# Value products of an attention kernel in 64-row tiles, put between the score products

## The chip, the cores and the metric

The kernel runs on one core of a Trainium2 chip. The metric is the device time of one execution in microseconds (us), the median of three runs. Profiled numbers come from one further execution, recorded by the hardware profiler.

## The reference, cut to what matters

One pre-norm transformer block on x of shape (8, 1024, 512), all float32: a differential attention and then a feed-forward part, each added to its input.

```python
# attention: b = 8, s = 1024, H = 16 heads, HD = 32
qkv = layernorm(x) @ w_qkv                       # (b, s, 1536)
q1, q2 = halves of q over d; k1, k2 likewise     # 16 numbers each
a1 = softmax(q1 @ k1.T * scale);  a2 = softmax(q2 @ k2.T * scale)
out = (a1 - lam * a2) @ v                        # per head, lam one number
out = out / rms(out) * norm_w * (1 - 0.8)
x = x + out.reshape(...) @ wo
# feed-forward, 512 -> 2048 -> 512; bitlinear: weights -1, 0, 1 with a scale for each row
y = layernorm(x)
h = bitlinear(y, w_fc) + gate * (y @ v.T @ fast_b.T @ u.T)
x = x + bitlinear(relu(h) ** 2, w_proj)
```

## The kernel before, in words

**Units and steps.** The attention is cut into 256 units: a batch entry, a head, and one half of the 1024 queries. A unit has 8 chunks `kc` of 128 keys, and the main loop (line 594) takes two chunks in a step, so a unit has four steps, with `kc` 0, 2, 4 and 6. The loop runs in an order written out by hand: `tc.manual_schedule` keeps each engine's instructions in the order in which the code gives them.

**What a step computes.** Both softmaxes of the differential attention are kept side by side: map 0 in rows 0 to 63 of the tiles of keys and queries, map 1 in rows 64 to 127. (The 16 numbers of a half head are split into high and low parts, which is how 64 rows come about.)

- `max_scores` (line 197) multiplies scores of a unit 16 chunks ahead, two products of 64 rows by 128 columns, into two of the three banks of `ps_mx`; VectorE reduces each bank to its row maximum (line 218, tile `nm`). A step has two such calls, so four products and four reductions.
- `exp_scores` (line 253) computes the scores of the present unit, transposed, keys by queries. For each map it takes two products into one bank: the negative maxima, spread by `one2` (tiles `nms`), and then keys by queries (`tk`, `tq`). ScalarE takes the exponential into `e` (line 273). A step has two such calls. The banks come from `ps_1` (tag `one`), which has four.
- `values` (line 296) multiplies the exponentials of the step before with the values `v`: four products side by side for each chunk, each 128 rows (keys) by 32 columns (the head's 32 numbers), for two maps and two quarters of queries, all in the one bank `acc`, which accumulates over the 8 chunks. `quarters` (line 287) issues them. The operands are plain float32, and each such product stands in the trace as two weight loads and two matmuls, so that the two calls of a step give 16 matmuls of `acc`.
- `evict` (line 305) brings a finished `acc` to `avs` with one ScalarE instruction, which also multiplies the rows of map 1 with minus lambda.

GpSimd adds the exponentials up (`add_up`, lines 283 and 285) for the softmax denominators.

**Work of 128 rows.** In the step with `kc` 0 there is more: `max_turn` (one transpose of the maxima, line 232, then two VectorE copies and DMAs to `nms`), `heads_out` (four transposes of `avs` of an earlier unit, line 324, then five VectorE instructions, lines 334 to 347), `sums` (the denominators, 16 matmuls of 128 rows by 32 columns through `quarters`, tile `one` from `es`), and mostly one piece of preparation for the next batch entry: `project` (8 matmuls of 128x128 by 512, line 157, then ScalarE line 164, VectorE line 165 and a store), `value_tile` (8 such matmuls, line 145, then ScalarE) or `turn_tile` (4 transposes). One step with `kc` 4 in four units has `output_rows` (line 383). All of these take a bank of `ps_1`.

**Order in a step, before.** TensorE does all score products, then the work of 128 rows, then the two `values` calls; what the other engines do with the results of the 128-row work (the `posts`) comes last, and `evict` comes at the start of the step after.

**Feed-forward.** After the units, four output banks `y` from `ps_1` and a work bank from `ps_acc` serve the feed-forward part.

Of the kernel before, what the change touches and what calls it, by code (L numbers as in the profile page):

```python
# [8 lines left out]
F32 = mybir.dt.float32  # L9
F32R = mybir.dt.float32r  # L10
AF = mybir.ActivationFunctionType
ALU = mybir.AluOpType
# [5 lines left out]
P = 128  # L18
# [6 lines left out]
def block_phases(  # L25
# [14 lines left out]
    nc = tc.nc  # L40
# [16 lines left out]
    p_tq = ctx.enter_context(tc.tile_pool(name="a_tq", bufs=5))  # L57
    wpool = ctx.enter_context(tc.tile_pool(name="a_w", bufs=1))
    ps_mx = ctx.enter_context(tc.tile_pool(name="a_ps_mx", bufs=3, space=PSUM))
    ps_1 = ctx.enter_context(tc.tile_pool(name="a_ps_1", bufs=4, space=PSUM))  # L60
    ps_acc = ctx.enter_context(tc.tile_pool(name="a_ps_acc", bufs=1, space=PSUM))

    wqk = big.tile([P, KC, 2 * E], F32, tag="wqk", name="wqk")
# [166 lines left out]
    def max_turn(u):  # L230
        tr = one_bank()
        nc.tensor.transpose(tr[0:8, 0:P], nm2_of.pop(u), ident)

        def post():
            mt = p_s.tile([8, 2, P], F32R, tag="mt", name="mt", bufs=2)
            nc.vector.tensor_copy(mt[:, 0, :], tr[0:8, 0:P])
            nc.vector.tensor_sub(mt[:, 1, :], tr[0:8, 0:P], mt[:, 0, :].bitcast(F32))
            md = dpool.tile([2, 4, 2, P], F32, tag="md", name="md", bufs=4)
            nc.sync.dma_start(md.rearrange("s c a t -> (s c) a t"), mt.bitcast(F32))
            for sm in range(2):  # L240
                nc.sync.dma_start(
                    nms[u % 3][64 * sm : 64 * sm + 2].bitcast(F32)
                    .rearrange("a (c t) -> a c t", c=4),
                    md[sm].rearrange("c a t -> a c t"),
                )

        return post
# [5 lines left out]
    def exp_scores(u, kc, between=None):  # L253


        if kc % 2 == 0:
            e_of[u, kc // 2] = p_e.tile([P, 2, 2, HS], F32, tag="e", name="e")
        e = e_of[u, kc // 2]
        halves = (1, 0) if between else (0, 1)
        st = {sm: one_bank() for sm in halves}  # L260
        for w, m, cols in (
            (one2, nms[u % 3], slice(0, P)),
            (tk_of[u // 2], tq_of[u], slice(kc * P, (kc + 1) * P)),
        ):
            for sm in halves:
                rows = slice(64 * sm, 64 * sm + 64)
                nc.tensor.matmul(  # L267
                    st[sm], w[rows, cols], m[rows, :], start=(w is one2), stop=(w is not one2)
                )
        if between:  # L270
            between()
        for sm in halves:
            nc.scalar.activation(e[:, kc % 2, sm, :], st[sm], AF.Exp)  # L273
# [13 lines left out]
    def quarters(out, w, e, start, stop):  # L287

        for g in range(4):
            nc.tensor.matmul(  # L290
                out[32 * g : 32 * g + 32, :], w,
                e[:, g // 2, (g % 2) * (HS // 2) : (g % 2 + 1) * (HS // 2)],
                start=start, stop=stop,
            )

    def values(u, kc):
        b, h = divmod(u // 2, H)
        if kc == 0:
            acc_of[u] = ps_acc.tile([P, 512], F32, tag="acc", name="acc")[:, 0 : HS // 2]
        quarters(  # L300
            acc_of[u], v_of[b][:, kc, h * HD : (h + 1) * HD], e_of[u, kc // 2][:, kc % 2],
            kc == 0, kc == NS - 1,
        )

    def evict(u):
        avs_of[u] = p_s.tile([P, 2, HS // 2], F32, tag="avs", name="avs", bufs=4)

        nc.scalar.activation(avs_of[u][:, 0, :], acc_of.pop(u), AF.Copy, scale=one_nlam)

    def sums(u):  # L310
        ps = one_bank()
# [121 lines left out]
    def whole(step):  # L433
        post = step()
        if post:
            post()
# [151 lines left out]
    for v in range(NU):  # L588
        adds.setdefault((v + 1, 2) if light(v) else (v + 2, 0), []).append(v)
        outs.setdefault((v + 2, 0) if light(v) else (v + 3, 0), []).append(v)  # L590
    done = None
    ctx.enter_context(tc.manual_schedule(engines=engines))
    with tc.tile_pool(name="a_e", bufs=5) as p_e, tc.tile_pool(name="a_es", bufs=2) as p_es:
        for s in range(0, NS * NU + 2, 2):
            u, kc = divmod(s, NS)
            um, im = divmod(s + AHEAD, NS)
            if done is not None:
                evict(done)
                done = None
            if u > NU - 2 * H and kc == 0:  # L600
                prep.fetch()
            if u == NU - 1 and kc == 0:

                m1 = nms[(NU - 3) % 3].rearrange("p (k r) -> p k r", k=KC)
                nc.sync.dma_start(
                    m1.bitcast(F32), prep.m1_d.rearrange("p k i r -> p k (i r)")
                )
            if um < NU:
                if im == 0 and um + 1 < NU:
                    if um % 2 == 1:  # L610
                        load_keys(um // 2 + 1)
                    load_queries(um + 1)
                between, first = max_scores(um, im, apart=True)
            else:
                between = first = None
            if u < NU:
                if u % (2 * H) == 0 and kc == 0:
                    assert not fill
                    fill = prepare(u // (2 * H) + 1) if u + 2 * H < NU else prepare_tokens()
                exp_scores(u, kc, between=between)  # L620
                if first:
                    first()
                exp_scores(u, kc + 1)
                add_up(u, kc)
            reduce = max_scores(um, im + 1) if um < NU else None
            posts = []

            if fill and (kc == 0 or kc == 4 and u % (2 * H) >= H and u % 4 == 0):
                prepare_step, long = fill.pop(0)
            else:  # L630
                prepare_step = None
            if prepare_step and long:
                posts.append(prepare_step())
            if kc == 0 and um <= NU:
                posts.append(max_turn(um - 1))
            for v in outs.pop((u, kc), []):
                posts.append(heads_out(v))
                if v % 4 == 3:
                    n = v // 4
                    later[u, 6] = lambda n=n: rms_squares(n)  # L640
                    later[u + 1, 0] = lambda n=n: rms_sums(n)
                    later[u + 1, 2] = lambda n=n: rms_apply(n)
                    later[u + 2, 4] = lambda n=n: output_rows(n)
            if (u, kc) in later:
                posts.append(later.pop((u, kc))())
            for v in adds.pop((u, kc), []):
                posts.append(sums(v))
            if prepare_step and not long:
                posts.append(prepare_step())
            if reduce:  # L650
                reduce()
            if 2 <= s < NS * NU + 2:
                uv, kv = divmod(s - 2, NS)
                values(uv, kv)
                values(uv, kv + 1)
                if kv == NS - 2:
                    done = uv
            for post in posts:
                if post:
                    post()  # L660
        evict(done)
        whole(lambda: sums(NU - 1))
    assert not later and list(adds.values()) == list(outs.values()) == [[NU - 1]]

# [45 lines left out]
        )  # L710

    def work_bank():
        return ps_acc.tile([P, 512], F32, tag="acc", name="wb")

    def turn(g, i):
        tr = work_bank().rearrange("p (k t) -> p k t", k=KC)
# [80 lines left out]
    for k in range(NG * NJ + LAG):  # L797
        g, j = divmod(k, NJ)
        if g < NG:
            if g + 1 < NG and j == 6:  # L800
                load(g + 1)
            if g + 1 < NG and 7 <= j < 9:
                stats(g + 1, 2 * j - 14)
                stats(g + 1, 2 * j - 13)
            if g + 1 < NG and 10 <= j < 14:
                center(g + 1, j - 10)
            post = hidden(g, j)
            if k == 0:
                first = post
            else:  # L810
                if k == 1:

                    r2_of[0] = first()
                r2_of[k] = post()
            if ends:
                ends.pop(0)()
            if k in rest:
                whole(rest.pop(k))
            if g + 1 < NG and 11 <= j < 15:
                turn(g + 1, j - 11)  # L820
            if g + 1 < NG and j == 15:
                low_rank(g + 1)
        if k >= LAG:
            gc, jc = divmod(k - LAG, NJ)
            if jc == 0:
                y_of[gc] = [ps_1.tile([P, E], F32, tag="one", name="y") for _ in range(4)]
            if k < NG * NJ:
                contract(y_of[gc], jc, r2_of.pop(k - LAG))
                if jc == NJ - 1:
                    output(gc, y_of.pop(gc))  # L830
# [283 lines left out]
```

## Time and profile before

| | |
|---|---|
| median of three runs | 5339.66 us (5339.15 to 5343.71) |
| span of the profiled execution | 5338.5 us |
| granted TensorE clock | 0.999 |
| TensorE matmul busy | 5280.1 us, 99% of the span |
| VectorE, ScalarE, GpSimd busy | 3787.7, 2832.5, 4121.0 us |
| matmuls of `acc` (line 290) | 16384, 1092.7 us busy |
| maxima (line 218), VectorE | 4096 of 683 ns |
| first and last score product of `max_scores` | 56.2 and 4226.5 us |

The profile lists busy time by engine, the chain of work that ended last, groups of instructions by source line, and a timeline. In the groups, "64*128 64x512" means a weight tile of 64 rows by 128 columns, through which 512 columns are streamed. PE is TensorE's matmuls, PEld its weight loads, DVE VectorE, ACT ScalarE, POOL GpSimd. A matmul's recorded duration includes its way through the array, so matmuls overlap in the record, and the distances between their starts say more than their durations.

### The profile page before, as it was taken

How to read it: one execution, taken by the hardware profiler on the slowest of the kernel's cores; microseconds unless marked ns; L12 is line 12 of the kernel's file. 1: busy time of each engine (PE TensorE's matmuls, PEld its weight loads, DVE VectorE, ACT ScalarE, POOL GpSimd, SP SyncE). 2: the span in 40 equal slices, each digit the busy share in tenths (PEclk: the TensorE clock that was granted, in tenths of full speed). 3: DMA queues.
4: the chain of work that ended last, by engine and by line, in shares of the span. 5: the costliest groups of instructions: out<-in, count | busy, mean ns of one | idle time of the engine just before them, and what ended most of it. 6: DMA issues, size and time to landing. Idle time of an engine off the chain costs nothing.

```text
span 5338.5 us, 105587 instructions
## 1 busy us (share of the span) xinstructions
PE 5280.1 (99%) x41522; PEld 3243.9 (61%) x41522; DVE 3787.7 (71%) x7599; ACT 2832.5 (53%) x5502; POOL 4121.0 (77%) x1495
## 2 busy tenths in 40 slices
PE   8999999999999999999999999999999999999999
PEld 4555555555555555555555555555555578888887
DVE  6877787777778777877777777777888645555554
ACT  4665566566656665666566656655666522222221
POOL 0898899889988998899899989998888733333333
PEclk9999999999999999999999999999999999999999
DMA  8112211211121112111211121112211101111111
GB/s 275 47 55 74 71 50 55 75 66 55 54 77 65 52 57 77 64 55 56 75 65 50 60 81 57 56 61 78 100 48 44 50 31 32 32 32 32 32 32 32
DMA packets 185246, 328.48 MB, mean 62 GB/s; under 512 B 33312, under 2 KB 55840, under 8 KB 184112
## 3 DMA queue, kind: packets, MB, share of 16 engines
q1 hardware_dynamic: 183824, 319.12, 18.3%
q8 instruction: 329, 5.39, 0.4%
q0 software_dynamic: 544, 2.10, 0.1%
q14 instruction: 165, 1.35, 0.1%
q10 hardware_dynamic: 384, 0.52, 0.0%
HBM read 209.16 MB, written 112.46 MB: 60 GB/s over the span
## 4 chain that ended last, share of the span: by engine, by line
PE 84%; POOL 11%; DVE 3%; issue 1%; ACT 1%; DMA 0%; SPq 0%; POOLq 0%; DVEq 0%; ACTq 0%
PE acc L290 15%; PE one L267 14%; PE mx L207 13%; PE y L763 9%; PE pf L744 8%; PE one L157 8%; POOL es L285 6%; PE one L290 4%; PE one L145 4%; PE one L383 3%; POOL es L283 3%; PE one L324 2%; DVE nm L218 1%; PE pf L748 1%; POOL ss L369 1%
## 5 line engine op out<-in xcount | busy, mean ns | idle before, releaser
L218 DVE TENSOR_REDUCE nm<-mx 128x1 f32<-128x512 f32 x4096 | 2550.3, 683 | 256.6 <-PE mx L207 251.5
L273 ACT ACTIVATE e<-one 128x512 f32<-128x512 f32 x4096 | 2116.5, 603 | 803.2 <-PE one L267 751.1
L285 POOL TENSOR_TENSOR es<-es,e 128x2048 f32<-128x2048 f32 x495 | 2261.3, 4568 | 63.2 <-ACT e L273 31.1
L207 PE MATMUL mx<-tk,tq 64*128 64x512 f32 x4096 | 1453.1, 444 | 6.2 <-DVE nm L218 5.6
L283 POOL TENSOR_TENSOR es<-e 128x2048 f32<-128x2048 f32 x256 | 1169.6, 4569 | 278.3 <-ACT e L273 278.2
L267 PE MATMUL one<-nms,one 64*128 64x512 f32 x4096 | 1175.8, 420 | 5.1 <-ACT e L273 2.7
L290 PE MATMUL acc<-e,v 128*32 128x256 f32 x16384 | 1092.7, 384 | 0.0
L207 PEld LDWEIGHTS mx<-tk,tq 64*128 64x128 f32 x4096 | 750.9, 184 | 549.0 <-DVE nm L218 312.3
L267 PE MATMUL one<-tq,tk 64*128 64x512 f32 x4096 | 1063.6, 392 | 0.0
L753 POOL TENSOR_TENSOR r<-r 128x512 f32<-128x512 f32 x256 | 268.4, 1050 | 639.2 <-ACT r L752 618.8
L290 PEld LDWEIGHTS acc<-e,v 128*32 128x32 f32 x16384 | 450.0, 109 | 433.7 <-issue 179.0
L267 PEld LDWEIGHTS one<-tq,tk 64*128 64x128 f32 x4096 | 580.2, 185 | 82.6
L752 ACT ACTIVATE r<-pf,s_fc 128x512 f32<-128x512 f32 x256 | 176.1, 688 | 794.6 <-PE pf L748 544.2
L267 PEld LDWEIGHTS one<-nms,one 64*128 64x128 f32 x4096 | 515.2, 184 | 80.5 <-DVE og L347 15.5
L763 PE MATMUL y<-wpr,r 128*128 128x512 f32 x2048 | 523.3, 397 | 3.7 <-DVE r L757 1.7
L756 DVE CAST r<-r 128x512 fp32r<-128x512 f32 x256 | 180.4, 705 | 425.9 <-POOL r L753 425.9
L157 PE MATMUL one<-hT,wqk 128*128 128x512 f32 x1024 | 475.4, 607 | 1.5 <-ACT hT L138 1.5
L763 PEld LDWEIGHTS y<-wpr,r 128*128 128x128 f32 x2048 | 375.0, 188 | 98.6 <-DVE o L773 20.1
L744 PE MATMUL pf<-hTh,wfc 128*128 128x512 f32 x1024 | 398.8, 389 | 0.0
L744 PE MATMUL pf<-hTl,wfc 128*128 128x512 f32 x1024 | 398.6, 389 | 0.0
L165 DVE SCALAR_TENSOR_TENSOR pc<-one,pc 128x512 fp32r<-128x512 f32 x128 | 88.5, 692 | 350.9 <-ACT pc L164 350.9
L157 PEld LDWEIGHTS one<-hT,wqk 128*128 128x128 f32 x1024 | 185.0, 190 | 217.3 <-issue 187.9
(137 smaller groups left out, 4284.1 us busy)
## 6 DMA issues: line engine op xcount, KB each, us to landing
qk<-pc SPq DMA_DIRECT2D x128, 512.0 KB
tq<-qk SPq DMA_DIRECT2D x512, 128.0 KB
tk<-qk SPq DMA_DIRECT2D x256, 256.0 KB
xs<-in_L_attn_x SPq DMA_DIRECT2D x64, 256.0 KB
xr<-in_L_attn_x SPq DMA_DIRECT2D x256, 64.0 KB
x_dram<-y SPq DMA_DIRECT2D x64, 256.0 KB
out<-o SPq DMA_DIRECT2D x248, 64.0 KB
nms<-md SPq DMA_DIRECT2D x512, 4.0 KB
```

The source lines that it names most:

```text
L145: nc.tensor.matmul(pv, hT_of[b][:, kc, c * P : (c + 1) * P], wv[:, kc, :], start=(kc == 0), stop=(kc == KC - 1),)
L157: nc.tensor.matmul(ps, wqk[:, kc, c0 : c0 + P], hT_of[b][:, kc, tok], start=(kc == 0), stop=(kc == KC - 1),)
L207: nc.tensor.matmul(mx[sm], tq[rows, c * P : (c + 1) * P], tk[rows, kh * 512 : kh * 512 + 512], start=True, stop=True,)
L218: nc.vector.tensor_reduce(nm_of[u][:, kh, sm, c : c + 1], mx[sm], AX.X, ALU.max, negate=True)
L267: nc.tensor.matmul(st[sm], w[rows, cols], m[rows, :], start=(w is one2), stop=(w is not one2))
L273: nc.scalar.activation(e[:, kc % 2, sm, :], st[sm], AF.Exp)
L283: nc.gpsimd.tensor_add(es_of[u], e_of[u, 0], e)
L285: nc.gpsimd.tensor_add(es_of[u], es_of[u], e)
L290: nc.tensor.matmul(out[32 * g : 32 * g + 32, :], w, e[:, g // 2, (g % 2) * (HS // 2) : (g % 2 + 1) * (HS // 2)], start=start, stop=stop,)
L744: nc.tensor.matmul(pf, w[:, kc, :], hT, start=(kc == 0 and i == 0), stop=False)
L753: nc.gpsimd.tensor_mul(r, r, r)
L763: nc.tensor.matmul(ys[i], r2[:, i * P : (i + 1) * P], prep.wpr[j // (NJ // 2)][:, j % (NJ // 2), :], start=(j == 0 and k == 0), stop=(j == ...
```

## The change

The value products are issued in tiles of 64 rows by 32 columns: each chunk's four products become eight, rows 0 to 63 into a bank `acc0`, rows 64 to 127 into a bank `acc1`. ScalarE brings `acc0` to SBUF as before, and one VectorE instruction for each unit adds `acc1`, times the same factor. The second bank is taken from `ps_1`, which has three instead of four. Within a step, the first chunk's value products now stand between the two `exp_scores` calls' products and the second chunk's after the last score products; the 128-row work comes after them, each piece with its own `post` right behind it, and `evict` comes before it. In the feed-forward part the fourth `y` bank is `acc0` and the work bank `acc1`.

```diff
-    ps_1 = ctx.enter_context(tc.tile_pool(name="a_ps_1", bufs=4, space=PSUM))
+    ps_1 = ctx.enter_context(tc.tile_pool(name="a_ps_1", bufs=3, space=PSUM))
...
     def values(u, kc):
         b, h = divmod(u // 2, H)
         if kc == 0:
-            acc_of[u] = ps_acc.tile([P, 512], F32, tag="acc", name="acc")[:, 0 : HS // 2]
-        quarters(
-            acc_of[u], v_of[b][:, kc, h * HD : (h + 1) * HD], e_of[u, kc // 2][:, kc % 2],
-            kc == 0, kc == NS - 1,
-        )
+            acc_of[u] = [
+                ps_acc.tile([P, 512], F32, tag=f"acc{r}", name=f"acc{r}")[:, 0 : HS // 2]
+                for r in range(2)
+            ]
+        e = e_of[u, kc // 2]
+        for g in range(4):
+            for r, acc in enumerate(acc_of[u]):
+                rows = slice(64 * r, 64 * r + 64)
+                nc.tensor.matmul(
+                    acc[32 * g : 32 * g + 32, :],
+                    v_of[b][rows, kc, h * HD : (h + 1) * HD],
+                    e[rows, kc % 2, g // 2, (g % 2) * (HS // 2) : (g % 2 + 1) * (HS // 2)],
+                    start=(kc == 0), stop=(kc == NS - 1),
+                )
 
     def evict(u):
         avs_of[u] = p_s.tile([P, 2, HS // 2], F32, tag="avs", name="avs", bufs=4)
-
-        nc.scalar.activation(avs_of[u][:, 0, :], acc_of.pop(u), AF.Copy, scale=one_nlam)
+        upper, lower = acc_of.pop(u)
+        av = avs_of[u][:, 0, :]
+        nc.scalar.activation(av, upper, AF.Copy, scale=one_nlam)
+        nc.vector.scalar_tensor_tensor(av, lower, one_nlam, av, ALU.mult, ALU.add)
...
         for s in range(0, NS * NU + 2, 2):
...
-            if done is not None:
-                evict(done)
-                done = None
...
+            uv, kv = divmod(s - 2, NS)
             if u < NU:
...
                 exp_scores(u, kc, between=between)
                 if first:
                     first()
+            if s >= 2:
+                values(uv, kv)
+            if u < NU:
                 exp_scores(u, kc + 1)
                 add_up(u, kc)
-            reduce = max_scores(um, im + 1) if um < NU else None
-            posts = []
-
+            if um < NU:
+                max_scores(um, im + 1)()
+            if s >= 2:
+                values(uv, kv + 1)
+                if kv == NS - 2:
+                    evict(uv)
+            todo = []
             if fill and (kc == 0 or kc == 4 and u % (2 * H) >= H and u % 4 == 0):
                 prepare_step, long = fill.pop(0)
+                if long:
+                    todo.append(prepare_step)
             else:
-                prepare_step = None
-            if prepare_step and long:
-                posts.append(prepare_step())
+                prepare_step, long = None, True
             if kc == 0 and um <= NU:
-                posts.append(max_turn(um - 1))
+                todo.append(lambda: max_turn(um - 1))
             for v in outs.pop((u, kc), []):
-                posts.append(heads_out(v))
+                todo.append(lambda v=v: heads_out(v))
...
             if (u, kc) in later:
-                posts.append(later.pop((u, kc))())
+                todo.append(later.pop((u, kc)))
             for v in adds.pop((u, kc), []):
-                posts.append(sums(v))
-            if prepare_step and not long:
-                posts.append(prepare_step())
-            if reduce:
-                reduce()
-            if 2 <= s < NS * NU + 2:
-                uv, kv = divmod(s - 2, NS)
-                values(uv, kv)
-                values(uv, kv + 1)
-                if kv == NS - 2:
-                    done = uv
-            for post in posts:
-                if post:
-                    post()
-        evict(done)
+                todo.append(lambda v=v: sums(v))
+            if not long:
+                todo.append(prepare_step)
+            for step in todo:
+                whole(step)
...
-        return ps_acc.tile([P, 512], F32, tag="acc", name="wb")
+        return ps_acc.tile([P, 512], F32, tag="acc1", name="wb")
...
-                y_of[gc] = [ps_1.tile([P, E], F32, tag="one", name="y") for _ in range(4)]
+                y_of[gc] = [ps_1.tile([P, E], F32, tag="one", name="y") for _ in range(3)]
+                y_of[gc].append(ps_acc.tile([P, E], F32, tag="acc0", name="y"))
```

More of the change, by code (lines that the diff above doesn't have):

```diff
@@ L596, in block_phases @@
             um, im = divmod(s + AHEAD, NS)
-            if done is not None:
-                evict(done)
-                done = None
             if u > NU - 2 * H and kc == 0:
```

## The prediction

> **What bounds the kernel now.** I read the page first, then TensorE's timeline of ordinary steps, then that of a step with 128-row work. The page's busy shares and its chain:
>
> ```profile
> PE 5280.1 (99%) x41522; PEld 3243.9 (61%) x41522; DVE 3787.7 (71%) x7599; ACT 2832.5 (53%) x5502; POOL 4121.0 (77%) x1495
> ...
> PE 84%; POOL 11%; DVE 3%; issue 1%; ACT 1%; DMA 0%; SPq 0%; POOLq 0%; DVEq 0%; ACTq 0%
> ```
>
> TensorE carries the end. But its busy time covers pauses, as a matmul's record runs on through the array. Starts tell more; one ordinary step on TensorE:
>
> ```profile
> 2001.17 0.50 PE L207 MATMUL mx<-tk,tq 64*128 64x512 f32 x1
> ...
> 2001.52 0.63 PE L267 MATMUL one<-tq,tk 64*128 64x512 f32 x2
> 2001.76 0.39 PE L207 MATMUL mx<-tk,tq 64*128 64x512 f32 x1
> ...
> 2002.46 0.50 PE L207 MATMUL mx<-tk,tq 64*128 64x512 f32 x2
> 2002.89 1.07 PE L290 MATMUL acc<-e,v 128*32 128x256 f32 x16
> 2003.89 0.50 PE L207 MATMUL mx<-tk,tq 64*128 64x512 f32 x1
> ```
>
> The step takes 2.72 us (other steps: 2.71). Its twelve score products run as six pairs, one in each half of the rows. Inside the group a pair takes 0.235 (2001.52 to 2001.76), the first takes 0.34, the last, up to the values, 0.43. So 0.1 is lost when the scores begin and 0.2 when they end. The last 0.2 has two parts, as the end of the attention shows, where no maxima remain:
>
> ```profile
> 4236.92 0.40 PE L267 MATMUL one<-tq,tk 64*128 64x512 f32 x2
> 4237.25 1.07 PE L290 MATMUL acc<-e,v 128*32 128x256 f32 x16
> 4238.25 0.50 PE L267 MATMUL one<-nms,one 64*128 64x512 f32 x2
> ```
>
> Here the last pair costs 0.33. The other 0.1 is the last `mx` product's weight load, which waits for a bank that VectorE frees late. Now a step with a projection, from its end:
>
> ```profile
> 2011.85 0.27 PE L232 MATMUL one<-ident,nm 128*8 128x128 f32 x1
> 2011.96 0.60 PE L324 MATMUL one<-ident,avs 128*128 128x128 f32 x4
> 2012.49 1.07 PE L290 MATMUL one<-es,ones 128*32 128x256 f32 x16
> 2013.38 1.05 PE L290 MATMUL acc<-e,v 128*32 128x256 f32 x16
> 2014.36 0.49 PE L207 MATMUL mx<-tk,tq 64*128 64x512 f32 x1
> ```
>
> Sixteen products of 128x32 take 0.89 when others of that shape follow (2012.49 to 2013.38), so 0.215 for a round of four side by side, after 0.025 for the first load. They take 0.98 to 1.00 when 64-row products follow, so leaving costs 0.12. And four transposes take 0.53 where 4 x 0.109 = 0.44 is the distance between their starts: 0.1 is lost between 128x128 and 128x32, **with the same rows and only the columns changed**. Every change of tile shape here is a stop: about 0.1 to empty the array, and then an uncovered weight load, 0.1 for 128 columns, 0.025 for 32.
>
> VectorE is near behind:
>
> ```profile
> 2001.71 2.48 DVE L218 TENSOR_REDUCE nm<-mx 128x1 f32<-128x512 f32 x4 [0.23 <-PE mx L207]
> ```
>
> An ordinary step cannot go below about 2.5 us by any change on TensorE.
>
> **The change part by part.** Baseline: the profiled execution's own 5338.5 us; the median, 5339.66, lies 1.2 above.
>
> *Streaming* costs nothing either way: twice as many value products, half as high, eight side by side instead of four. Two chunks are four rounds of 0.215 as before, if the eight do run together. The trace shows four columns together and two row halves together, not both; the bounds are four rounds (two halves of `mx` and `one` start within 0.01, nearest row) and eight. I take four. In the trace the starts within a round lie 6 to 7 ns apart, so a round of eight ends 0.03 later.
>
> *Tile shapes in an ordinary step.* Before: scores, values. After: three pairs, one chunk's values, three pairs, the other's: twice as many changes. No row shows 64x128 to 64x32. From below, it is free, being the same rows; from above, it costs what the rows show. I take the rows, because the change of columns alone (transposes to `sums`) stops TensorE as the change of rows does. Half a step is then 0.34 + 0.235 + 0.33 for the pairs (0.33, not 0.43: `mx` products come spread out, so their bank is free in time) and 0.24 + 0.215 + 0.12 + 0.03 = 0.605 for the values. That makes 1.51, a step 3.0, **0.29 more than 2.71**. There are 768 steps without `kc` 0 among the 1024: 223 us.
>
> Here a rule of the Trainium skill bears on the case. "TensorEngine Tiling (Array Packing)", section Key Properties, says that changing the tiling mode drains the TensorE, and that going to another tile of the mode does not; 64x128 and 64x32 stand there as two modes. That speaks against this change, and extends what I read off the rows to the pair of shapes that no row has, but it gives no duration. By the rule the sum stands; without it, the first rival's sum would hold.
>
> *The 256 steps with `kc` 0.* Before: scores to work 0.2 + 0.1, work to `sums` 0.12, `sums` to values nothing, values to scores 0.22: 0.66 in all, counting the load waits. After: scores to values 0.13, back 0.25, again 0.13, values to work 0.2, work to `sums` 0.12, back 0.22: 1.05. That is 0.4 more, 102 us.
>
> *One bank fewer, and posts right behind their work.* Before, a step's banks of `one` go round four: two `exp_scores` calls take all four, the projection, `max_turn`, `heads_out` and `sums` the next four. With three, `sums` takes the projection's bank and the next step's first two score banks are those of `max_turn` and `heads_out`. How late they come free:
>
> ```profile
> 2012.05 0.60 ACT L164 ACTIVATE pc<-one 128x512 fp32r<-128x512 f32 x1 [2.54 <-PE one L157]
> ```
>
> ```profile
> 2012.68 0.69 DVE L165 SCALAR_TENSOR_TENSOR pc<-one,pc 128x512 fp32r<-128x512 f32 x1 [3.06 <-ACT pc L164]
> ...
> 2014.73 0.29 DVE L347 TENSOR_TENSOR og<-one,o 128x128 f32<-128x128 f32 x1
> ```
>
> The projection's bank is free at 2013.37, the `heads_out` bank at 2015.02. `sums` started at 2012.49; it would now wait 0.9. It then takes 1.0, the scores start at 2014.4, and their second pair, due at 2014.76, waits 0.3 for the `heads_out` bank. Queued behind on TensorE is everything else, scores included, so ScalarE and VectorE wait too. 1.24 for 91 projections in such steps (13 of 16 in each of seven batches): 113 us. The 56 value tiles have no VectorE evict: 0.2 each, 11. In the other steps, `max_turn` follows the values at once, and VectorE has the last two reductions, the new addition and 1.75 for `max_turn` and `heads_out` (2013.29 to 2015.02) to do, while TensorE needs only 0.7 of transposes, 1.0 of `sums` and 0.34: about 0.9 waiting in 28 such steps, 0.6 where four more transposes lie between (49), and some 14 in the last batch: 67 us. Together 190. The bounds are 0, if the posts find VectorE early, and 250, if its queue runs late.
>
> *The rest.* VectorE's addition (256 of about 0.4, half of line 165's 0.69 with a little over) stays inside steps of 3.0 with 2.5 of reductions; uncovered it would be 100 us. ScalarE's evict moves ahead of the projection's, and the accumulator banks are free long before the next unit's values, a work block later; without that block they would cost some 0.5 for a unit. GpSimd gets more time, not more work. The feed-forward part has the same number of banks: 0. The DMA issues of the posts move with them by under 2 us, and their data is due a unit later.
>
> Sum: 5338.5 + 223 + 102 + 190 = 5853.5, with 1.2 for the median **5855 us**.
>
> **The rivals.** *A: equal rows do not stop.* If 64x128 and 64x32 products follow each other freely, a step streams 6 x 0.235 + 4 x 0.215 = 2.27 and VectorE's 2.48 sets it: 0.2 less in 768 steps, and 0.2 less in the 256 others (0.66 falls to 0.5, the late load goes): 5135. With 190 of bank waits 5325; I put it at 5230. It decides for faster once a change of shape costs under 0.05. Against it: the 0.1 between transposes and `sums`. For it: no row has this pair.
>
> *B: the eight tiles do not run together.* Each step has four rounds more, 0.86, or 880 us in 1024 steps: 6735. For it: each matmul is two passes of plain float32, and the score pairs that do run together are single passes. Against it: nothing in the pairs or fours shows a limit; a round of four passes in 0.215.
>
> *C: the banks come free in time,* the stops as forecast: 5339 + 325 = 5665.
>
> **How the numbers follow.** Forecast 0.76, own range 5690 (stops of 250, waits of 100) to 6020 (rounds of eight at 0.24, which is 100 more, and waits of 250); C 0.08; A 0.11; B 0.05. The range 5580 to 6060 takes in the forecast and C, and leaves out A, B and the forecast's edges. A measurement of this kernel can tell some 0.2% (11 us) from no change. Faster: most of A, 0.09. Same: 0.02, where A's gain and the waits cancel. Slower: 0.89.
>
> **What would show it.** In TensorE's timeline: ordinary steps of 3.0 us, the first pair after each `acc0`/`acc1` group at 0.34, the groups 0.6 long, their weight loads never ahead of the last score product. In the steps with a projection: weight loads of `sums` waiting for `pc` on VectorE by 0.9, and of `nms` products for `og` by 0.3 or more. VectorE's `nm` reductions idle 0.5 in each step. Steps near 2.5 with loads ahead of time would prove A, groups of 1.0 or more for one chunk B.

## The result and the profile after

The changed kernel takes **5799.56 us** (median of four, 5798.54 to 5800.95) against 5341.53 for the kernel before in the same comparison: ratio **1.0858**, 95% interval 1.0843 to 1.0874, 458 us slower. The forecast was 5855, its range 5580 to 6060. The page of the profiled execution (span 5798.7 us), busy shares and chain:

```profile
PE 5640.7 (97%) x57906; PEld 2930.0 (51%) x57906; DVE 3937.4 (68%) x7855; ACT 2904.7 (50%) x5502; POOL 4122.7 (71%) x1495
...
PE 87%; ACT 4%; DVE 3%; issue 3%; POOL 1%; DMA 0%; SPq 0%; DVEq 0%; POOLq 0%; ACTq 0%
```

TensorE still carries the end, and GpSimd, with the same work in a longer span, is down to 1% of the chain. The 16384 matmuls more are the value products' doubling; what they stream is the same. An ordinary step on TensorE's timeline:

```profile
2375.61 0.50 PE L207 MATMUL mx<-tk,tq 64*128 64x512 f32 x1
...
2375.95 0.62 PE L267 MATMUL one<-tq,tk 64*128 64x512 f32 x2
2376.18 0.39 PE L207 MATMUL mx<-tk,tq 64*128 64x512 f32 x1
2376.50 0.66 PE L307 MATMUL acc<-e,v 64*32 64x256 f32 x16
2377.10 0.50 PE L267 MATMUL one<-nms,one 64*128 64x512 f32 x2
...
2377.66 0.40 PE L207 MATMUL mx<-tk,tq 64*128 64x512 f32 x2
2377.99 0.66 PE L307 MATMUL acc<-e,v 64*32 64x256 f32 x16
2378.58 0.50 PE L207 MATMUL mx<-tk,tq 64*128 64x512 f32 x1
```

The step is 2.97 us, 0.27 more than the 2.71 before. Each half reads as forecast: 0.34 to the second pair (2375.61 to 2375.95), 0.23 to the third, 0.32 from there to the values (2376.18 to 2376.50), 0.60 from values to scores. Sixteen 64x32 matmuls take the time of two rounds of eight, so all eight run side by side. VectorE, which had 0.23 idle in a step, has half a microsecond:

```profile
2375.12 2.48 DVE L218 TENSOR_REDUCE nm<-mx 128x1 f32<-128x512 f32 x4 [0.49 <-PE mx L207]
```

A step with a projection, from its end on:

```profile
2329.84 0.27 PE L232 MATMUL one<-ident,nm 128*8 128x128 f32 x1
2329.95 0.60 PE L335 MATMUL one<-ident,avs 128*128 128x128 f32 x4
2331.51 1.07 PE L290 MATMUL one<-es,ones 128*32 128x256 f32 x16 [0.96 <-DVE pc L165]
2332.51 0.50 PE L207 MATMUL mx<-tk,tq 64*128 64x512 f32 x1
2332.51 1.04 PE L267 MATMUL one<-nms,one 64*128 64x512 f32 x2
2333.06 0.72 PE L267 MATMUL one<-tq,tk 64*128 64x512 f32 x2
```

From the transposes to `sums` there are 1.56 us, 0.53 before: `sums` waits 1.03 for the bank that VectorE's line 165 empties, and the second score pair starts 0.55 after the first instead of 0.34. Its weight load shows for what it waits:

```profile
2333.06 0.18 PEld L267 LDWEIGHTS one<-nms,one 64*128 64x128 f32 x1 [0.37 <-ACT avs L327]
```

Line 327 is ScalarE's copy of the denominators out of the bank of `sums`. Steps with a projection go from 7.75 to 9.18, and the ordinary step after them from 2.74 to 3.30 (medians, as for all kinds of steps below, from the distances between the steps' first score products in the trace).

### The profile page after: what moved, and what is told of

Its sections match the earlier page's. It is cut to its first block, busy times and chain, and to the rows that moved or that the text cites. A ratio compares the mean times of both kernels' runs of the same rounds, so it can differ in the third digit from the quotient of the medians.

```text
span 5798.7 us, 138697 instructions
## 1 busy us (share of the span) xinstructions
PE 5640.7 (97%) x57906; PEld 2930.0 (51%) x57906; DVE 3937.4 (68%) x7855; ACT 2904.7 (50%) x5502; POOL 4122.7 (71%) x1495
## 4 chain that ended last, share of the span: by engine, by line
PE 87%; ACT 4%; DVE 3%; issue 3%; POOL 1%; DMA 0%; SPq 0%; DVEq 0%; POOLq 0%; ACTq 0%
PE one L267 21%; PE acc L307 20%; PE mx L207 10%; PE one L157 7%; PE y L768 7%; PE pf L749 7%; PE one L290 4%; PE one L145 4%; PE one L394 4%; DVE pc L165 1%; ACT avs L327 1%; ACT e L273 1%; ACT pc L164 1%; PE pf L753 1%; ACT v L149 1%
## 5 line engine op out<-in xcount | busy, mean ns | idle before, releaser
L218 DVE TENSOR_REDUCE nm<-mx 128x1 f32<-128x512 f32 x4096 | 2602.9, 684 | 538.4 <-PE mx L207 514.9
L273 ACT ACTIVATE e<-one 128x512 f32<-128x512 f32 x4096 | 2223.9, 595 | 1054.1 <-PE one L267 1042.1
L307 PE MATMUL acc<-e,v 64*32 64x256 f32 x32768 | 1360.1, 389 | 0.0
L267 PE MATMUL one<-nms,one 64*128 64x512 f32 x4096 | 1324.3, 477 | 29.1 <-DVE og L358 11.3
L207 PE MATMUL mx<-tk,tq 64*128 64x512 f32 x4096 | 1338.2, 421 | 1.7 <-DVE nm L218 1.0
L207 PEld LDWEIGHTS mx<-tk,tq 64*128 64x128 f32 x4096 | 581.0, 184 | 486.4 <-issue 356.9
L307 PEld LDWEIGHTS acc<-e,v 64*32 64x32 f32 x32768 | 371.5, 105 | 742.8 <-issue 742.1
L267 PEld LDWEIGHTS one<-tq,tk 64*128 64x128 f32 x4096 | 553.9, 186 | 33.0
L290 PE MATMUL one<-es,ones 128*32 128x256 f32 x4096 | 274.1, 384 | 99.4 <-DVE pc L165 84.2
```

The source lines that it names most:

```text
L207: nc.tensor.matmul(mx[sm], tq[rows, c * P : (c + 1) * P], tk[rows, kh * 512 : kh * 512 + 512], start=True, stop=True,)
L218: nc.vector.tensor_reduce(nm_of[u][:, kh, sm, c : c + 1], mx[sm], AX.X, ALU.max, negate=True)
L267: nc.tensor.matmul(st[sm], w[rows, cols], m[rows, :], start=(w is one2), stop=(w is not one2))
L290: nc.tensor.matmul(out[32 * g : 32 * g + 32, :], w, e[:, g // 2, (g % 2) * (HS // 2) : (g % 2 + 1) * (HS // 2)], start=start, stop=stop,)
L307: nc.tensor.matmul(acc[32 * g : 32 * g + 32, :], v_of[b][rows, kc, h * HD : (h + 1) * HD], e[rows, kc % 2, g // 2, (g % 2) * (HS // 2) : ( ...
```

## The experiments

**One part alone: the place, in the kernel before.** The first chunk's products, 128x32, go between the two `exp_scores` calls. Nothing else changes.

```diff
                 if first:
                     first()
+            if s >= 2:
+                uv, kv = divmod(s - 2, NS)
+                values(uv, kv)
+            if u < NU:
                 exp_scores(u, kc + 1)
...
-                uv, kv = divmod(s - 2, NS)
-                values(uv, kv)
                 values(uv, kv + 1)
```

> The kernel before with one thing done: the first chunk's value products, 128x32 as they are, stand between the two calls of score products. Four banks, one accumulator bank, the 128-row work ahead of the second chunk's value products and posts last, all as before. Theory of stops: ordinary steps 2.93 instead of 2.71, 165 us over 749 steps, and 0.25 in the 256 steps with kc 0, 64 us, less some 20 to 30 that VectorE's late posts cost before and that longer steps hide: 5545 us. Rival (the stop is paid only together with the turned order): under 5450 us.

Measured 5505.77 us, ratio 1.0304 (1.0287 to 1.0321), 163 us slower than the kernel before. TensorE's timeline of an ordinary step:

```profile
2228.12 0.49 PE L207 MATMUL mx<-tk,tq 64*128 64x512 f32 x1
...
2228.70 0.39 PE L207 MATMUL mx<-tk,tq 64*128 64x512 f32 x1
2229.02 0.64 PE L290 MATMUL acc<-e,v 128*32 128x256 f32 x8
2229.59 0.50 PE L267 MATMUL one<-nms,one 64*128 64x512 f32 x2
...
2230.15 0.40 PE L207 MATMUL mx<-tk,tq 64*128 64x512 f32 x2
2230.48 0.64 PE L290 MATMUL acc<-e,v 128*32 128x256 f32 x8
2231.05 0.49 PE L207 MATMUL mx<-tk,tq 64*128 64x512 f32 x1
```

The step is 2.93, and the gap from the last score pair to the values, 0.32 to 0.33, is the one that 64x32 products have in the changed kernel. A change of rows and columns (64x128 to 128x32) and one of columns alone (64x128 to 64x32) stop TensorE alike. The steps with `kc` 0 lost less than expected: with a projection or a value tile 7.75 became 7.96, but those with `turn_tile` or nothing long stayed within 0.02.

**128x32 products in the new places.** Everything else as in the changed kernel, first with three banks of `one`, then with four.

```diff
-            acc_of[u] = [ ... two banks ... ]
-        ... eight products of 64x32, and evict with VectorE's addition
+            acc_of[u] = ps_acc.tile([P, 512], F32, tag="acc0", name="acc0")[:, 0 : HS // 2]
+        quarters(
+            acc_of[u], v_of[b][:, kc, h * HD : (h + 1) * HD], e_of[u, kc // 2][:, kc % 2],
+            kc == 0, kc == NS - 1,
+        )
...
+        nc.scalar.activation(avs_of[u][:, 0, :], acc_of.pop(u), AF.Copy, scale=one_nlam)
```

With three banks:

> The changed kernel with the value products as before in shape, four of 128x32 for a chunk in one bank, evicted by ScalarE alone, but in their new places between the score products; three banks of one, order and posts as changed. Theory of stops, the same for a change of rows and of columns: two rounds less wide by 0.03 each, an ordinary step 2.92 us, 5745 us. Rival (equal rows do make a change cheaper, only not free): 0.1 us more at each of four changes, 0.4 in a step, over 6100 us. Rival (eight side by side or VectorE's addition cost something): below 5700 us.

Measured 5729.4 us, ratio 1.0719 (1.0703 to 1.0735). The height of the tiles, with its second bank and its addition, costs 70 us and saves nothing at the changes of shape: ordinary steps are 2.95, not 3.3.

With the fourth bank (`bufs=3` to `bufs=4`, and the feed-forward part's banks as in the kernel before):

> As the one with 128x32 value products in their new places, but with the fourth bank of one given back. It differs from that one in the bank alone. Theory of banks as forecast: the waits of sums (1.03 after a projection, 0.29 after a value tile) and of the next step's second score pair go, 130 to 160 us less than that kernel, about 5600 us, and ordinary steps stay. Rival (the waits come from posts queued on VectorE, whatever the banks): less than 40 us between the two.

Measured 5581.34 us, ratio 1.0443 (1.0428 to 1.0459), 148 us below three banks. The same place in the two timelines, three banks first:

```profile
2275.14 0.60 PE L323 MATMUL one<-ident,avs 128*128 128x128 f32 x4
2276.70 1.07 PE L290 MATMUL one<-es,ones 128*32 128x256 f32 x16 [0.96 <-POOL es L285]
```

```profile
2200.62 0.60 PE L323 MATMUL one<-ident,avs 128*128 128x128 f32 x4
2201.15 1.07 PE L290 MATMUL one<-es,ones 128*32 128x256 f32 x16
```

With one bank more the 1.03 is gone. The releaser named with three banks, GpSimd, is the profile's inference for a wait on two engines; only the bank differs, so it was the bank.

**VectorE's addition left out.** The lower 64 keys of each chunk are then missing from the result; all else runs.

```diff
-        nc.vector.scalar_tensor_tensor(av, lower, one_nlam, av, ALU.mult, ALU.add)
```

> The changed kernel without VectorE's addition of the second accumulator bank: the lower 64 keys' share of each chunk is left out of the value products' result, everything else runs. If the 70 us between 64x32 and 128x32 products in the same places are the wider rounds (0.03 at two places in 1024 steps, some 35 to 60), little goes: 5770 to 5800 us. If they are VectorE's addition (256 of 0.48 us, in the steps with kc 0, where VectorE's queue is longest), 35 to 70 us go: 5730 to 5765 us.

Measured 5758.62 us, ratio 1.078 (1.0764 to 1.0796), 41 us below the changed kernel: a third of the addition's busy time in the changed kernel's groups,

```profile
L319 DVE SCALAR_TENSOR_TENSOR avs<-acc,one_nlam,avs 128x256 f32<-128x256 f32 x256 | 123.9, 484 | 18.9 <-ACT avs L318 18.7
```

comes through. It shows where `turn_tile` or nothing long stands: a step with `turn_tile` falls from 5.35 to 5.20 and the one after it from 3.48 to 3.15, the one after a step with nothing long from 3.73 to 3.45, while those with a projection stay at 9.18. Some 29 of the 70 us are left, by difference, for the wider rounds and the second bank.

**Both chunks' products together again, with three banks.** First 64x32 in the changed kernel:

```diff
-            if s >= 2:
-                values(uv, kv)
             if u < NU:
                 exp_scores(u, kc + 1)
                 add_up(u, kc)
...
             if s >= 2:
+                values(uv, kv)
                 values(uv, kv + 1)
```

> The changed kernel with both chunks' value products together after the last score products: 64x32 tiles, two banks and the order of the 128-row work stay. Theory of stops (each change of tile shape costs 0.12 to 0.25 us, and the change doubled their number): an ordinary step falls from 2.975 to 2.73 us (that of before plus 0.03 for the wider rounds), which is 183 us over 749 steps, and the steps with kc 0 lose 0.28 each, 70 us: 5545 us. Theory of banks (the three banks and the posts carry the loss): the place of the value products matters little, over 5700 us.

Measured 6238.76 us, ratio 1.1673 (1.1656 to 1.169): far slower, where both theories had it faster or about as it was ("over 5700" holds in the letter only). An ordinary step on TensorE, and the leading entry of its loads in the list of waits:

```profile
2584.05 0.39 PE L267 MATMUL one<-nms,one 64*128 64x512 f32 x1
2584.73 0.49 PE L267 MATMUL one<-nms,one 64*128 64x512 f32 x1 [0.29 <-ACT e L273]
2584.74 0.72 PE L267 MATMUL one<-tq,tk 64*128 64x512 f32 x2
2585.07 0.62 PE L207 MATMUL mx<-tk,tq 64*128 64x512 f32 x2
2585.62 1.09 PE L307 MATMUL acc<-e,v 64*32 64x256 f32 x32
2586.64 0.50 PE L207 MATMUL mx<-tk,tq 64*128 64x512 f32 x1
```

```profile
PEld one L267 <- ACT e L273: 713.8, 1027, 1.2
```

The values behave as expected (1.02 from 2585.62 to 2586.64). But the second `exp_scores` call's second bank is the first call's first, and ScalarE empties it 0.68 after it is wanted. Value products between the two calls, 0.60 in the changed kernel, cover nearly that time. The expectation had counted changes of shape and forgotten this.

To see that it is the bank and not the tiles, the same with 128x32 products in one accumulator bank:

> As the one before it, with three banks of one. The run of 64x32 products together in the kernel with three banks took 6239 us, with score products waiting 0.69 for ScalarE in each step. Theory (three banks starve a closed group of score products, whatever the value tiles are): the same wait here, ordinary steps 3.38, in all 6190 us. Rival (the wait came from the 64-row tiles or the second accumulator bank): ordinary steps 2.71 and under 5550 us.

Measured 6159.79 us, ratio 1.153 (1.151 to 1.1549), ordinary steps 3.38. The waits carry the same entry:

```profile
PEld one L267 <- ACT e L273: 710.0, 1028, 1.0
```

**Together, with four banks,** the new order of the 128-row work kept (`bufs=4` beside the last edit):

> 128x32 value products in one bank, both chunks together after the last score products, four banks of one; the order of the 128-row work (behind the values, posts right behind their work) stays as changed. Against the kernel with the same products between the scores and four banks it differs in the place alone. Theory of stops: ordinary steps go from 2.93 back to 2.71 and the steps with kc 0 lose 0.25, 230 us: 5350 us, and what is left above the kernel before is the price of the new order of the 128-row work. Rival (the place is free, the posts carry the loss): above 5500 us.

Measured 5454.89 us, ratio 1.0209 (1.0194 to 1.0224), 126 us below the same products between the scores and 113 above the kernel before. That lies between the two theories (5350, and over 5500). Ordinary steps are back at 2.71, but the step after a projection takes 3.60 (2.74 before). TensorE and VectorE in that step:

```profile
2140.33 0.50 PE L207 MATMUL mx<-tk,tq 64*128 64x512 f32 x1
...
2141.34 0.39 PE L267 MATMUL one<-nms,one 64*128 64x512 f32 x1
2142.02 0.49 PE L267 MATMUL one<-nms,one 64*128 64x512 f32 x1 [0.28 <-ACT e L273]
```

```profile
2141.56 0.29 DVE L346 TENSOR_TENSOR og<-one,o 128x128 f32<-128x128 f32 x1
2141.77 2.47 DVE L218 TENSOR_REDUCE nm<-mx 128x1 f32<-128x512 f32 x4
```

TensorE's largest loss is the 0.68 from 2141.34 to 2142.02: the second `exp_scores` call waits for a bank that ScalarE's exponential of the same step empties, and it does so in each of the 91 steps after a projection, though the tag has four banks. VectorE is late in that step as well: it reads the `heads_out` bank until 2141.85 and comes to the maxima 1.4 after the scores' start. That its queue keeps the fourth bank from serving is an inference; no run takes the two apart. In the kernel before, the value products stand between the 128-row work and the next scores, and VectorE works most of its queue off under them. So the order costs, too: 113 us here, but 76 between the first run (5505.77) and the one with the products apart and four banks (5581.34), where stops make the steps longer.

**The 128-row work turned: `sums` first, the long piece last.** First in the changed kernel:

```diff
-                if long:
-                    todo.append(prepare_step)
...
+            for v in adds.pop((u, kc), []):
+                todo.append(lambda v=v: sums(v))
             if kc == 0 and um <= NU:
                 todo.append(lambda: max_turn(um - 1))
...
-            for v in adds.pop((u, kc), []):
-                todo.append(lambda v=v: sums(v))
-            if not long:
-                todo.append(prepare_step)
+            if prepare_step:
+                todo.append(prepare_step)
```

> The changed kernel with the order of the 128-row work turned: sums first, then max_turn, heads_out and the later pieces, and the projection, value tile or transposes last; three banks. No piece then takes the bank of one that was evicted just before. Theory of banks: sums no longer waits, nor does the next step's second pair after a projection or a value tile: 1.3 in 91 steps and 0.6 in 56, 150 us less, 5650 us, ordinary steps as they are. Rival (order does not matter, VectorE's queue does): 5780 us or more.

Measured 5665.34 us, ratio 1.0598 (1.0581 to 1.0616), 134 us below the changed kernel:

```profile
2230.56 1.07 PE L290 MATMUL one<-es,ones 128*32 128x256 f32 x16
...
2232.12 3.70 PE L157 MATMUL one<-hT,wqk 128*128 128x512 f32 x8
2235.75 0.50 PE L207 MATMUL mx<-tk,tq 64*128 64x512 f32 x1
2235.76 0.73 PE L267 MATMUL one<-nms,one 64*128 64x512 f32 x2
2236.09 0.62 PE L267 MATMUL one<-tq,tk 64*128 64x512 f32 x2
```

`sums` follows the values at once, the second pair starts 0.34 after the first, and steps with a projection take 8.17. So most of what three banks cost here, 134 us next to the 148 of the bank, goes with another order of the pieces.

The same order in the best of the variants, 128x32 products together and four banks:

> 128x32 value products together, four banks, and sums directly behind them, then max_turn, heads_out, the later pieces and the projection, value tile or transposes last. sums has the values' shape, so that the step with kc 0 changes shape three times, as in the kernel before. Theory of stops: 0.06 to 0.1 us less than with sums at the end in 256 steps, 5330 us, as fast as the kernel before or faster by up to 15 us; the two VectorE posts then come later in steps without long work, which can cost 0.4 in some 50 steps, so no more than 5360 us.

Measured 5470.57 us, ratio 1.024 (1.0225 to 1.0255): 16 us slower than with `sums` last, not faster. Steps with a projection fell from 7.89 to 7.65, but steps after `turn_tile` rose from 3.06 to 3.98. None of the variants beats the kernel before.

## Why the prediction was right, step by step

The runs make a ladder from one kernel to the other, each rung one difference: the place of the products, 163 us (before to 5505.77); the turned order of the 128-row work with its posts, 76 (to 5581.34); one bank fewer, 148 (to 5729.4); 64x32 tiles, 70 (to 5799.56), of which the addition 41. They add up to 457 us, of the 458 measured. Each rung holds for its place on the ladder only: with the products together, the same bank is worth 705 (5454.89 to 6159.79), and taking 128x32 products apart costs 126 with four banks but saves 430 with three (6159.79 to 5729.4).

Summed over the steps of the two traces, with 0.27 for the stops of a step without `kc` 0, the prediction's terms come out so (an estimate): stops in those steps some 205 for 223, stops in steps with `kc` 0 some 65 for 102, waits for banks after projections and value tiles some 150 for 124, waits after the other steps some 40 for 67.

- *Streaming:* right, the lower bound. Sixteen 64x32 matmuls take 0.60 with the stop behind them.
- *Stops in an ordinary step:* right in kind and size, 0.27 for 0.29, so some 205 us over 768 steps for 223. (The prediction's two halves of 1.51 make 3.02, which is 0.31 more than before and not 0.29.) From the last score pair to the values 0.32 to 0.33 pass where pairs among themselves take 0.23, with 64x32 products as with 128x32. The Trainium skill's rule that a changed tiling mode drains the TensorE ("TensorEngine Tiling (Array Packing)", Key Properties) agrees with this 0.1 for 64x128 to 64x32. But "every change of tile shape" was too wide: `max_turn`'s product of 128x8 stands between products of 128x128, and the first transpose follows it after 0.11 (2329.84 to 2329.95), the distance that transposes have among themselves.
- *Steps with `kc` 0:* this term, 0.4 in all 256 steps, is over-sized. It holds with a projection (9.18 less 7.75 less the 1.03 of waiting) and with a value tile. A step with nothing long grew by 0.2, and with `turn_tile` by 0.2 of which 0.15 is a wait for a bank. There TensorE waited before the change already: from `max_turn` to the transposes 0.27 passed (2217.46 to 2217.73 in the timeline of before), where 0.11 pass after the change; the new stops fell partly into that. The two terms of stops together are about 270 us instead of 325, and that is about the whole miss of 55.
- *Banks:* `sums` waits 1.03 for 0.9 after a projection, on VectorE's line 165 as forecast, and 0.29 for 0.2 after a value tile. The next step's second pair waits 0.2 for 0.3, but the prediction had the wrong bank: it named that of `heads_out`, emptied by VectorE's `og`, and the load waits for ScalarE's copy of `sums` after each of the 91 projections and 56 value tiles; for `og` it waits after 42 of 49 steps with `turn_tile`. The simple rotation that the prediction assumed is not what the trace shows, and the 0.2 is near the 0.3 by luck. (Its 0.9 and 0.3 make 1.2, not 1.24.) The fourth bank is worth 148 with 128x32 products, which have no addition.
- *The addition:* its own term was put at nothing, "inside steps of 3.0"; it costs 41. The cover named was VectorE's slack in ordinary steps, but the addition falls in the steps with `kc` 0, ahead of the `max_turn` and `heads_out` instructions that empty banks. The term for banks did count it in VectorE's queue for steps without long work, 67 us, and that is where leaving it out shows. The 148 and the 41 make 189, so the 190 came out right in sum, with the part after projections and value tiles too small and the part after other steps too large; that these cancel is luck.
- *Turned order:* had no price of its own apart from the stops and banks; with four banks it costs 113 where ordinary steps are short and 76, one stop in each `kc` 0 step included, where they are long.

Rival A falls with the rows of the result and with the 128x32 products, which are not dearer in the same places. B falls with the rounds. C falls by the waits for banks, 148 us of which the fourth bank takes away.

## What to carry to other kernels

Count the changes of tile shape along TensorE's order, not only the streamed columns, and price each from starts in the timeline; here a value tile with the rows of the score tiles did not make the change cheaper (steps of 2.97 against 2.95). Before a PSUM bank is spent, look up in the trace which bank each piece's load waits for and which engine empties it, since a rotation worked out by hand named the wrong one here; the order of the pieces can be worth nearly as much as the bank (134 and 148 us). A term is hidden only if its own place in the queue has slack, so look up the step in which it falls.

## What was not expected of the hardware

Nothing in single durations. The surprise was in the interplay: with three banks, closing the score products up costs 439 us (5799.56 to 6238.76) although it takes out two stops in each step, since ScalarE's 0.6 us exponentials then hold the bank that TensorE wants.
